# Twelve more contexts' keys and values computed inside level 0's self attention, early contexts spread over the batch, and level 3's steps reordered

## The chip, the core and the metric

The kernel runs on one core of one Trainium2 chip. The metric is device time in microseconds (us) for one execution of the whole program. The core has five engines, each with its own instruction sequence: TensorE (PE in the profile, with its weight loads as PEld), VectorE (DVE), ScalarE (ACT), GpSimd (POOL) and SyncE (SP, which here issues DMA transfers). They wait for one another by semaphores. Everything is computed in single precision, but for a few small whole-number tables.

## The reference

The program is a stack of four levels over 2048 rows of x (64 batch elements, called contexts below after the 64 context sequences they attend to, with 32 rows each) and a context of 257 rows per batch element, all 256 wide. Each level attends to the context (xattn), then to itself (attn), then has a feed-forward part (ffn):

```
B, T, S, D = 64, 32, 257, 256
x    [64, 32, 256]     ctx  [64, 257, 256]
x = l0_xattn(x, ctx); x = l0_attn(x); x = l0_ffn(x)
x = l1_xattn(x, ctx); x = l1_attn(x); x = l1_ffn(x)
x = l2_xattn(x, ctx); x = l2_attn(x); x = l2_ffn(x)
x = l3_xattn(x, ctx); x = l3_attn(x); x = l3_ffn(x)
```

Three parts matter here.

- Level 3's cross attention: for each batch element, k = ctx Wk + bk and v = ctx Wv + bv; queries from a layer norm of x; per head (16 heads of width 16) softmax(q k / 4) v, a projection, and a residual sum. The keys and values depend on the context and on weights alone, not on x, so they can be computed at any earlier time.
- Level 0's self attention: 16 heads of width 16 over the 32 rows of a batch element, with queries and keys of unit length, softmax, output projection, residual sum.
- Level 0's feed-forward: a mixture of eight experts in which each expert takes the 256 rows with the highest router probability.

## The kernel before

x stays in SBUF as 16 tiles of 128 rows (NT = 16), each holding four batch elements (NB = 4). The parts run one after the other; a scheduler orders instructions by their dependences and by memory, except within `as_written(...)`, where the named engines keep the order in which the code issues them.

**Early and late contexts.** Level 3's keys and values take four pieces of matmul work per context: two for keys (each 128x257 out), two for values (each 128x256 out). `l3_keys_values(one, ps, n)` (L1027) sets up a generator that does this for the next n contexts: it loads the weights `kv_w` (two DMAs on SP, L1033), loads each context's transpose (SP, L1042), and yields after every piece. ACT moves the pieces from PSUM to SBUF (L1056 and L1065) and issues the DMA that writes the finished keys and values to DRAM (`self.kv[b]`, 513 KB, L1066). `filled(n)` (L1071) runs the next n pieces, so that they stand in the gaps of whatever calls it. The generator is set up twice, for 16 contexts each: in level 0's feed-forward (L1169) and in level 1's feed-forward (L1655). Contexts 0 to 31 are therefore "early"; level 3 reads their keys and values back from DRAM. Contexts 32 to 63 are "late": level 3 loads the context and does the four pieces itself.

**Level 0's self attention** (`l0_attn`, L795) is a software pipeline over the 16 tiles, in which one iteration runs steps of several tiles: norm and query/key/value projection of tile i or i+1, unit length and `heads_first` of tile i-1 (four transposes into PSUM `m`; ACT copies them to `qT` and `kb`), `scores` and softmax of tile i-2 (PSUM `s`, four banks; DVE reads them twice, for the row maxima `hs_m` and for the difference `hs_e`), and `weighted` and `output` of tile i-3 (PSUM `o`). Its PSUM pool has one buffer of `m`, two of `qk`, one of `s` (four banks) and one of `o`, eight banks in all. The steps of all four compute engines are kept as written.

**Level 0's feed-forward** (`l0_ffn`, L1152) begins with eight DMAs of 1 MB on SP for the experts' weights (`w_all`, L1162) and with `probabilities` (L998): for each of 16 tiles a layer norm to `rt_n` (four buffers), a DMA of it to DRAM (`nd`), two transposes, a small matmul with the router's weights, and one `filled()`. Then `places` (L1108) finds each expert's 256th highest probability bit by bit, in 30 steps of compare, count on PE (`pl_m`), and a few small DVE operations, with one `filled()` a step and six behind. Only DVE keeps its written order in this whole part, and PE, DVE and ACT keep it within the 30 steps.

**Level 3's cross attention** (`l3_xattn`, L2641) is again a software pipeline, one context per iteration n, with PE, DVE and ACT kept as written. `loaded` brings keys and values or the context; `norm`, `turned` and `projected` make the queries for four contexts at a time; `scores` (PSUM `s`) is followed by the negative row maxima `nm` (DVE, L2788) and the exponentials `e` with their sums `ss` (ACT, L2789); `divided` takes `rs` = 1/`ss` (DVE, L2797) and multiplies (POOL, L2798); `keys_first` transposes e, evacuated as `eT` half by DVE and half by ACT; `weighted` multiplies with the values, and DVE picks and sums the own heads' part (`t`, `oT`, L2825 and L2831); `last_rows` and `output` finish a tile. `keys_values` does the four pieces of a late context.

Of the kernel before, what the change touches and what calls it, by code (L numbers as in the profile page):

```python
# [26 lines left out]
B, T, S, D = 64, 32, 257, 256  # L27
NT = B * T // 128
NB = 4
KP, KC = 96, 3  # L30
KL = S - 2 * KP
SP = KP * KC
# [291 lines left out]
class Perceiver:  # L324
    def __init__(self, ctx, tc, a):
        self.tc, self.nc, self.a = tc, tc.nc, a
        nc = self.nc
        self.n_tiles = 0
        self.const = ctx.enter_context(tc.tile_pool(name="const", bufs=1))
        self.wpool = ctx.enter_context(tc.tile_pool(name="weights", bufs=N_SLOTS))  # L330
        self.x = self.sb(self.const, [128, NT, D], "x")
        self.cols = self.sb(self.const, [128, N_COL], "cols")
        self.con = self.sb(self.const, [128, N_CON], "con")
        nc.sync.dma_start(self.cols, a["cols"])
        self.ident = self.sb(self.const, [128, 128], "ident")
        make_identity(nc, self.ident)
        self.neg_half = self.sb(self.const, [128, 1], "neg_half")
        nc.gpsimd.memset(self.neg_half, -0.5)
        self.seed = self.sb(self.const, [128, 1], "seed", I32)
        nc.gpsimd.memset(self.seed, RSQRT_SEED + 1)  # L340

        self.ctx_st = self.sb(self.const, [128, 2 * B, 6], "ctx_st")
        self.ctx_st_x = self.sb(self.const, [B, 1, 6], "ctx_st_x")


        self.k_wT = self.sb(self.const, [128, 6, D], "k_wT")
        self.c_mean = self.sb(self.const, [128, B, 2], "c_mean")
        self.c_rc = self.sb(self.const, [128, B, 2], "c_rc")
        self.nxT = self.sb(self.const, [128, 2, B], "nxT")
        dram = ctx.enter_context(tc.tile_pool(name="rows_d", bufs=1, space=bass.MemoryType.DRAM))  # L350
        self.abd = self.sb(dram, [B, 2, S], "abd")

        self.kv = self.sb(dram, [B, 128, 2 * S + 2 * D], "kv")
        self.n_kv = 0

    def forms(self, pool):
# [438 lines left out]
    def l0_attn(self):  # L795
        nc, tc, a = self.nc, self.tc, self.a
        wqkv = self.weight(a["l0a_wqkv"], 2)
        wo = self.weight(a["l0a_wo"], 4)
        with ExitStack() as st:
# [12 lines left out]
            def norm_1(i):  # L812
                st = self.sb(pool, [128, 6], "ln_st")
                nc.vector.bn_stats(st, self.x[:, i, :])
                mv = self.sb(pool, [128, 2], "ln_mv")
                nc.vector.bn_aggr(mv, st)
                t_n[i] = mv, self.rsqrt(pool, mv[:, 1:2], LN_EPS, "ln_r")
# [104 lines left out]
            def output(i):  # L922
                py = self.sb(ps, [128, D], "o")
                self.mm(py, [(t_o[i][:, k, :], wo[:, k, :]) for k in range(4)])
                nc.vector.tensor_tensor(self.x[:, i, :], self.x[:, i, :], py, ALU.add)

            norm_1(0), norm_2(0), turned(0)
            st.enter_context(self.as_written(nc.tensor, nc.vector, nc.scalar, nc.gpsimd))
            for i in range(NT + 3):
                steps = [  # L930
                    (i + 1, norm_1),
                    (i - 1, unit),
                    (i, projected),
                    (i, lambda t: lengths(t, 0)),
                    (i - 2, scores),
                    (i + 1, norm_2),
                    (i - 3, weighted),
                    (i - 1, heads_first),
                    (i - 2, divided),
                    (i, lambda t: lengths(t, 1)),  # L940
                    (i - 3, output),
                    (i + 1, turned),
                    (i - 2, diagonal),
                ]
                for t, step in steps:
                    if 0 <= t < NT and not (t == 0 and step in (norm_1, norm_2, turned)):
                        step(t)

    def heads_softmax(self, pool, src, bd, scale, plus=0.0):

# [73 lines left out]
        nc.vector.tensor_tensor(p, lg, bcast(ss, 2, 8), ALU.mult)  # L1024
        return p

    def l3_keys_values(self, one, ps, n):  # L1027


        nc, a = self.nc, self.a  # L1030
        w = self.sb(one, [128, 2, 2, D], "kv_w")
        for j in range(2):
            nc.sync.dma_start(w[:, j], a["l3x_w"][1 + j].rearrange("p (k n) -> p k n", k=2))  # L1033
        wk, wv = w[:, 0], w[:, 1]
        todo = range(self.n_kv, self.n_kv + n)
        self.n_kv += n
        ts = {}

        def loaded(b):
            if b in todo:  # L1040
                t = self.sb(self.wpool, [128, 2048], "w")
                nc.sync.dma_start(t[:, 0 : 2 * S], a["ctxT"][b])  # L1042
                ts[b] = t

        def steps():
            for b in todo[:2]:
                loaded(b)
            for b in todo:
                loaded(b + 2)
                t = ts.pop(b)  # L1050
                cT = t[:, 0 : 2 * S].rearrange("p (k s) -> p k s", k=2)
                kv = t[:, 2 * S : 4 * S + 2 * D]
                for o in range(2):
                    pk = self.sb(ps, [128, S], "h")
                    self.mm(pk, [(wk[:, k, o * 128 : (o + 1) * 128], cT[:, k, :]) for k in range(2)])
                    nc.scalar.activation(  # L1056
                        kv[:, o * S : (o + 1) * S], pk, AF.Identity, bias=self.col("L3_xattn_bk", o)
                    )
                    yield
                pv = self.sb(ps, [128, 2, D], "y")  # L1060
                for c in range(2):
                    self.mm(pv[:, c, :], [(cT[:, k, c * 128 : (c + 1) * 128], wv[:, k, :]) for k in range(2)])
                    if c == 0:
                        yield
                nc.scalar.copy(kv[:, 2 * S :], pv.rearrange("p c f -> p (c f)"))  # L1065
                nc.scalar.dma_start(self.kv[b], kv)  # L1066
                yield

        self.between = steps()
# [82 lines left out]
    def l0_ffn(self):  # L1152
        nc, tc, a = self.nc, self.tc, self.a
        wg = self.weight(a["l0f_wg"], 2)
        with ExitStack() as st:
# [10 lines left out]
            rows = st.enter_context(tc.tile_pool(name="l2r", bufs=1))  # L1166
            one1 = st.enter_context(tc.tile_pool(name="l0s", bufs=1))
            pool = st.enter_context(tc.tile_pool(name="l0f", bufs=3))
            self.l3_keys_values(one1, ps, 16)  # L1169
            p = self.probabilities(one, pool, ps, wg, None, nd)  # L1170
            st.enter_context(self.as_written(nc.vector))
            place = self.places(one, pool, ps, tab, p)
# [462 lines left out]
    def l1_ffn(self, ahead, last):  # L1635
# [4 lines left out]
        with ExitStack() as st:  # L1640
# [11 lines left out]
            sums = self.sb(dram, [NT * 128, D], "sums")  # L1652
            nc.scalar.dma_start(sums.rearrange("(i p) f -> p i f", p=128), self.x)
            xn = self.sb(dram, [NT * 128, R], "xn")
            self.l3_keys_values(one, ps, 16)  # L1655
            p = self.probabilities(one, pool, ps, wr, br, xn)
            nc.scalar.dma_start(xn.rearrange("(i p) f -> p i f", p=128)[:, :, D:R], p)
            place = self.places(one, pool, ps, tab, p)
# [982 lines left out]
    def l3_xattn(self):  # L2641
# [3 lines left out]
        with ExitStack() as st:  # L2645
# [100 lines left out]
                    )  # L2746

            def loaded(b):
                kv = self.sb(pool, [128, 2 * S + 2 * D], "kv", bufs=7)
                t_kv[b] = [kv[:, 0 : 2 * S].rearrange("p (k s) -> p k s", k=2), kv[:, 2 * S :].rearrange("p (c f) -> p c f", c=2)]  # L2750
                if b < self.n_kv:
                    nc.sync.dma_start(kv, self.kv[b])
                    return
                cT = self.sb(pool, [128, 2, S], "cT", bufs=4)
                nc.sync.dma_start(cT, a["ctxT"][b].rearrange("p (k s) -> p k s", k=2))
                t_c[b] = cT

            def keys_values(b):
                if b < self.n_kv:
                    return  # L2760
                cT = t_c[b]
                kT, v = t_kv[b]
                for o in range(2):
                    pk = self.sb(ps, [128, S], "m")
                    self.mm(pk, [(wk[:, k, o * 128 : (o + 1) * 128], cT[:, k, :]) for k in range(2)])
                    nc.scalar.activation(kT[:, o, :], pk, AF.Identity, bias=self.col("L3_xattn_bk", o))
                pv = self.sb(ps, [128, 2, D], "m")
                for c in range(2):
                    self.mm(pv[:, c, :], [(cT[:, k, c * 128 : (c + 1) * 128], wv[:, k, :]) for k in range(2)])
                nc.vector.tensor_copy(v, pv)  # L2770

            def scores(b):
# [9 lines left out]
                            [(qb[f, c, bl].rearrange("p h t -> p (h t)"), kT[f, c, :])],  # L2782
                        )
                nm = self.sb(pool, [128, 4], "nm")
                e = self.sb(pool, [128, 4, S], "e")
                ss = self.sb(pool, [128, 4], "ss")
                for r in range(4):
                    nc.vector.tensor_reduce(nm[:, r : r + 1], pss[r], AX.X, ALU.max, negate=True)  # L2788
# [44 lines left out]
                )  # L2833

            st.enter_context(self.as_written(nc.tensor, nc.vector, nc.scalar))
            for n in range(-5, B + 6):

                steps = [(loaded, n + 3, 1), (norm, n + 4, NB), (scores, n, 1), (keys_values, n + 1, 1)]
                steps += [(divided, n, 1), (turned, n + 3, NB), (projected, n + 2, NB)]
                steps += [(weighted, n - 2, 1), (keys_first, n - 1, 1), (last_rows, n - 4, NB), (output, n - 8, NB)]  # L2840
                if n == -4:
                    row_values()
                for step, at, per in steps:
                    if at % per == 0 and 0 <= at < B:
                        step(at // per)
# [95 lines left out]
```

## Time and profile before

| | us |
|---|---|
| median of 3 runs | 3927.5 |
| lowest and highest of them | 3921.29, 3932.42 |
| the profiled execution | 3939.03 |
| its span in the profile | 3937.3 |

The mean granted TensorE clock of the profiled execution is 0.955 of full speed. Over the span the engines are busy as follows:

| engine | busy us | share |
|---|---|---|
| PE | 3546.4 | 90% |
| PEld | 2794.3 | 71% |
| DVE | 1963.4 | 50% |
| POOL | 1387.9 | 35% |
| ACT | 1293.2 | 33% |

The parts that the change touches stand in these stretches of the span: level 0's self attention from 388 to 588 us, level 0's feed-forward up to its expert slots from 588 to 694 us, and level 3's cross attention from about 3190 to 3595 us.

How to read it: a timeline line gives start and length in us, the engine, the line of the code, the operation, what it writes and reads by the program's names with its shape, and how many such instructions were joined (x4). A bracket at the end gives how long the engine had been idle before, and what released it. One matmul of single precision shows as two or more records. In a table of windows each engine's busy time is followed by its number of records, and PEclk is the clock granted to TensorE as a share of full speed. A busy share over the whole span averages stages with different limits, so each stage is looked at by itself.

### The profile page before, as it was taken

How to read it: one execution, taken by the hardware profiler on the slowest of the kernel's cores; microseconds unless marked ns; L12 is line 12 of the kernel's file. 1: busy time of each engine (PE TensorE's matmuls, PEld its weight loads, DVE VectorE, ACT ScalarE, POOL GpSimd, SP SyncE). 2: the span in 40 equal slices, each digit the busy share in tenths (PEclk: the TensorE clock that was granted, in tenths of full speed). 3: DMA queues.
4: the chain of work that ended last, by engine and by line, in shares of the span. 5: the costliest groups of instructions: out<-in, count | busy, mean ns of one | idle time of the engine just before them, and what ended most of it. 6: DMA issues, size and time to landing. Idle time of an engine off the chain costs nothing.

```text
span 3937.3 us, 74907 instructions
## 1 busy us (share of the span) xinstructions
PE 3546.4 (90%) x29677; PEld 2794.3 (71%) x29677; DVE 1963.4 (50%) x5180; ACT 1293.2 (33%) x3551; POOL 1387.9 (35%) x1752
## 2 busy tenths in 40 slices
PE   7999778879899789799999899979999987998998
PEld 5788446756577667577777566669999965776776
DVE  5555665234344441677766466632222246554454
ACT  2333223423233132333333243322222235543332
POOL 5433751133311113555655244451121135333121
PEclk9999889989999889899999899999999989999999
DMA  6342007256100265333333000010000133110000
GB/s 211 124 153 87 8 7 257 89 188 208 50 2 2 80 184 166 107 91 84 86 85 93 25 1 2 23 66 1 1 1 1 44 102 101 37 42 22 7 7 12
DMA packets 176413, 281.11 MB, mean 71 GB/s; under 512 B 33536, under 2 KB 109824, under 8 KB 171840
## 3 DMA queue, kind: packets, MB, share of 16 engines
q1 hardware_dynamic: 155472, 239.58, 19.7%
q10 hardware_dynamic: 14976, 25.01, 1.8%
q0 software_dynamic: 5616, 11.74, 1.3%
q8 instruction: 236, 3.87, 0.4%
q14 instruction: 113, 0.93, 0.1%
HBM read 243.46 MB, written 32.79 MB: 70 GB/s over the span
## 4 chain that ended last, share of the span: by engine, by line
PE 72%; DVE 11%; POOL 6%; ACT 5%; issue 3%; DMA 2%; ACTq 0%; SPq 0%; DVEq 0%; POOLq 0%
PE m L471 32%; PE p L471 10%; PE s L471 5%; PE y L471 3%; PE h L471 3%; PE b L471 3%; PE o L471 3%; PE ab L471 2%; ACT e L2789 2%; DVE bd L970 2%; PE y L476 2%; PE k L471 1%; PE c L471 1%; POOL e L2798 1%; PE m L465 1%
## 5 line engine op out<-in xcount | busy, mean ns | idle before, releaser
L471 PE MATMUL m<-w,oT 128*128 128x256 f32 x1152 | 272.8, 387 | 23.4 <-ACT eT L2809 15.2
L471 PEld LDWEIGHTS m<-w,oT 128*128 128x128 f32 x1152 | 219.9, 194 | 63.1 <-ACT eT L2809 17.0
L471 PE MATMUL m<-nTg,w 128*128 128x256 f32 x1024 | 234.7, 387 | 4.3 <-ACT k L1520 2.9
L471 PEld LDWEIGHTS m<-nTg,w 128*128 128x128 f32 x1024 | 193.3, 192 | 35.6 <-ACT k L1520 4.9
L2798 POOL TENSOR_TENSOR e<-e,rs 128x1028 f32<-128x1028 f32 x64 | 121.7, 1902 | 200.2 <-DVE rs L2797 200.2
L471 PE MATMUL s<-cT,ut 128*128 128x257 f32 x768 | 181.1, 386 | 0.0
L471 PE MATMUL m<-pT,cn 128*128 128x384 f32 x512 | 176.2, 487 | 2.5 <-DVE pT L2174 2.5
L2151 ACT ACTIVATE p<-s,bi 128x257 f32<-128x257 f32 x192 | 88.9, 472 | 247.0 <-DVE bi L2147 226.7
L423 POOL TENSOR_SCALAR ln_r_v<-ln_mv 128x1 f32<-128x1 f32 x176 | 38.7, 223 | 348.1 <-DVE ln_mv L454 266.3
L471 PEld LDWEIGHTS s<-cT,ut 128*128 128x128 f32 x768 | 143.5, 193 | 19.4 <-ACT p L2151 0.2
L2789 ACT ACTIVATE e<-s,nm 128x257 f32<-128x257 f32 x256 | 118.1, 474 | 113.4 <-DVE nm L2788 93.1
L970 DVE STREAM_TRANSPOSE bd<-hs_p 32x512 f32<-32x512 f32 x192 | 134.8, 702 | 40.2 <-POOL hs_p L964 37.0
L2120 POOL TENSOR_TENSOR cT<-cT,ab 128x514 f32<-128x514 f32 x64 | 82.4, 1288 | 205.4 <-PE m L471 85.8
L471 PEld LDWEIGHTS m<-pT,cn 128*128 128x128 f32 x512 | 96.5, 189 | 58.7 <-DVE pT L2174 2.9
L2255 POOL TENSOR_TENSOR sr<-ss,neg_half 128x16 f32<-128x16 f32 (+1 forms) x33 | 95.0, 2879 | 113.1 <-DVE ss L2253 113.1
L471 PE MATMUL m<-w,nT 128*128 128x512 f32 (+2 forms) x320 | 126.2, 536 | 8.8 <-ACT nT L829 8.2
L2545 POOL TENSOR_TENSOR tB<-hB 128x512 f32<-128x512 f32 x8 | 10.2, 1271 | 326.2 <-ACT hB L2583 326.2
L471 PE MATMUL ab<-nTg,w 128*128 128x256 f32 x512 | 117.1, 388 | 6.5 <-DVE hA L2561 5.5
L471 PE MATMUL m<-w,nTg 128*128 128x512 f32 x256 | 117.7, 604 | 0.0
L471 PEld LDWEIGHTS ab<-nTg,w 128*128 128x128 f32 x512 | 98.2, 194 | 23.3 <-DVE hA L2561 9.2
L2160 POOL TENSOR_TENSOR p<-p,rs 128x771 f32<-128x771 f32 x64 | 95.2, 1488 | 46.7 <-DVE rs L2159 27.9
L471 PE MATMUL o<-bd,v 128*64 128x128 f32 (+1 forms) x1536 | 90.1, 287 | 21.4 <-DVE bd L970 21.4
(712 smaller groups left out, 8819.9 us busy)
## 6 DMA issues: line engine op xcount, KB each, us to landing
ct<-in_ctx SPq DMA_DIRECT2D x192, 256.0 KB
cT<-in_ctxT SPq DMA_DIRECT2D x32, 1028.0 KB
cT<-in_ctxT SPq DMA_DIRECT2D x96, 257.0 KB
ab<-abd SPq DMA_DIRECT2D x64, 257.0 KB
kv<-w ACTq DMA_DIRECT2D x32, 513.0 KB
kv<-kv SPq DMA_DIRECT2D x32, 513.0 KB
rb<-rd SPq DMA_DIRECT2D x16, 514.0 KB
w<-in_ctxT SPq DMA_DIRECT2D x32, 257.0 KB
```

The lines of the kernel that those rows point to most:

```text
L423: nc.gpsimd.tensor_scalar(t, src, eps, None, ALU.add)
L465: self.nc.tensor.transpose(out[:, c, :], src[:, c * 128 : (c + 1) * 128], self.ident)
L471: self.nc.tensor.matmul(out, lhsT=l, rhs=r, start=j == 0, stop=j == last)
L476: self.nc.tensor.matmul(out[:, 0:n], lhsT=cT[0], rhs=self.k_qm[:, 0, 0:n], start=True, stop=False)
L970: self.nc.vector.transpose(bd[q, :, b, :], p[q])
L2120: nc.gpsimd.tensor_tensor(cT, cT, bcast(ab[:, 0, :], 1, 2), ALU.mult)
L2151: nc.scalar.activation(p[:, g, :], pss[g], AF.Exp, bias=bi[:, g : g + 1], accum_out=ss[:, g : g + 1])
L2160: nc.gpsimd.tensor_tensor(p, p, bcast(rs, 2, S), ALU.mult)
L2255: nc.gpsimd.tensor_tensor(r, ss, self.neg_half[:p].to_broadcast([p, nh]), ALU.pow)
L2545: nc.gpsimd.tensor_tensor(t1, b12, b11, ALU.subtract)
L2789: nc.scalar.activation(e[:, r, :], pss[r], AF.Exp, bias=nm[:, r : r + 1], accum_out=ss[:, r : r + 1])
L2798: nc.gpsimd.tensor_tensor(e, e, bcast(rs, 2, S), ALU.mult)
```

## The change

- Instead of the first 32, 44 contexts are early, and they are spread over the batch: of each 16, all but the numbers 0, 3, 6, 9 and 12. Twenty contexts stay late.
- The 12 additional ones are done within `l0_attn`. The pieces take the scores' PSUM banks `s` (one tile of four banks for a context: two for keys, one for both value pieces) and four SBUF buffers `kv_t` of that part. Each iteration runs two pieces after `heads_first`, one after `output` and one after `turned`, for i = 1 to 12.
- `l3_keys_values` gets its PSUM banks and its buffers from the caller. The two places that had it keep their own banks (`h`, `h`, `y`) and 16 contexts each.
- In `l3_xattn` the order of the steps changes: `weighted` and `keys_first` go ahead of `divided` and are done one iteration later, as are `last_rows` and `output`; the loop is two iterations longer. There are eight buffers of `kv` in place of seven and four of `e` in place of three.

The order of instructions that results also differs where no line of the diff stands: `l0_attn` takes more memory, and the start of `l0_ffn`, which had run within it (four `rt_n` and their writes to `nd`, and the DMAs of `kv_w`), comes after it; `kv_w` stands on SP behind the eight loads of `w_all`, and 16 of the pieces that stood one per tile in `probabilities` stand together between the first and the second step of `places`.

```diff
+EARLY = 44
+        self.early = [b for b in range(B) if (b + 1) * EARLY // B > b * EARLY // B]
...
+            banks = {}
+            def bank(j):
+                if j == 0:
+                    banks["s"] = self.sb(ps, [128, 4, 512], "s")
+                return banks["s"][:, j, :]
+            self.l3_keys_values(
+                one, 12, bank, lambda: self.sb(one, [128, 4 * S + 2 * D], "kv_t", bufs=4)
+            )
             norm_1(0), norm_2(0), turned(0)
...
                     (i - 1, heads_first),
+                    (i - 1, lambda t: self.filled(2)),
                     (i - 2, divided),
                     (i, lambda t: lengths(t, 1)),
                     (i - 3, output),
+                    (i - 1, lambda t: self.filled(1)),
                     (i + 1, turned),
+                    (i - 1, lambda t: self.filled(1)),
                     (i - 2, diagonal),
...
+            self.filled(4 * B)
...
-    def l3_keys_values(self, one, ps, n):
+    def l3_keys_values(self, one, n, bank, buf=None):
...
-        todo = range(self.n_kv, self.n_kv + n)
+        todo = self.early[self.n_kv : self.n_kv + n]
...
-                    pk = self.sb(ps, [128, S], "h")
+                    pk = bank(o)[:, 0:S]
...
-                pv = self.sb(ps, [128, 2, D], "y")
+                pv = bank(2)
...
-            self.l3_keys_values(one1, ps, 16)
+            self.l3_keys_values(one1, 16, lambda j: self.sb(ps, [128, 512], "hhy"[j]))
...
-                kv = self.sb(pool, [128, 2 * S + 2 * D], "kv", bufs=7)
+                kv = self.sb(pool, [128, 2 * S + 2 * D], "kv", bufs=8)
...
-                if b < self.n_kv:
+                if b in self.early:
...
-                e = self.sb(pool, [128, 4, S], "e")
+                e = self.sb(pool, [128, 4, S], "e", bufs=4)
...
-            for n in range(-5, B + 6):
+            for n in range(-5, B + 8):
                 steps = [(loaded, n + 3, 1), (norm, n + 4, NB), (scores, n, 1), (keys_values, n + 1, 1)]
-                steps += [(divided, n, 1), (turned, n + 3, NB), (projected, n + 2, NB)]
-                steps += [(weighted, n - 2, 1), (keys_first, n - 1, 1), (last_rows, n - 4, NB), (output, n - 8, NB)]
+                steps += [(turned, n + 3, NB), (projected, n + 2, NB), (weighted, n - 3, 1)]
+                steps += [(keys_first, n - 2, 1), (divided, n, 1), (last_rows, n - 5, NB), (output, n - 9, NB)]
```

More of the change, by code (lines that the diff above doesn't have):

```diff
@@ L1039, in loaded @@
         def loaded(b):
[L1040 to L1043, printed above, removed]
+            t = buf() if buf else self.sb(self.wpool, [128, 2048], "w")
+            nc.sync.dma_start(t[:, 0 : 2 * S], a["ctxT"][b])
+            ts[b] = t
         def steps():
@@ L1047, in steps @@
                 loaded(b)
-            for b in todo:
-                loaded(b + 2)
+            for at, b in enumerate(todo):
+                for c in todo[at + 2 : at + 3]:
+                    loaded(c)
                 t = ts.pop(b)
@@ L1059, in steps @@
                     yield
-                pv = self.sb(ps, [128, 2, D], "y")
+                pv = bank(2)
                 for c in range(2):
-                    self.mm(pv[:, c, :], [(cT[:, k, c * 128 : (c + 1) * 128], wv[:, k, :]) for k in range(2)])
+                    self.mm(
+                        pv[:, c * D : (c + 1) * D],
+                        [(cT[:, k, c * 128 : (c + 1) * 128], wv[:, k, :]) for k in range(2)],
+                    )
                     if c == 0:
                         yield
-                nc.scalar.copy(kv[:, 2 * S :], pv.rearrange("p c f -> p (c f)"))
+                nc.scalar.copy(kv[:, 2 * S :], pv)
                 nc.scalar.dma_start(self.kv[b], kv)
@@ L1654, in l1_ffn @@
             xn = self.sb(dram, [NT * 128, R], "xn")
-            self.l3_keys_values(one, ps, 16)
+            self.l3_keys_values(one, 16, lambda j: self.sb(ps, [128, 512], "hhy"[j]))
             p = self.probabilities(one, pool, ps, wr, br, xn)
@@ L2758, in keys_values @@
             def keys_values(b):
-                if b < self.n_kv:
+                if b in self.early:
                     return
```

## The prediction, made before the changed kernel had run

> **What bounds the kernel now.** I began with the chain of waits over the whole span, to see which engine sets the end, and then cut the span into the stages that the change touches.
>
> ```profile
> PE 72%; DVE 11%; POOL 6%; ACT 5%; issue 3%; DMA 2%; ACTq 0%; SPq 0%; DVEq 0%; POOLq 0%
> ```
>
> TensorE carries 72% of the chain, so matmuls taken out of one stage and put into another pay only where the first stage is bound by TensorE and the second is not. The table of windows says which is which; its columns are length, busy PE, weight load, DVE, ACT and POOL, granted clock, DMA share, GB/s.
>
> ```profile
> 388.00:588.00 200.00, 144.47 (x1896) 94.41 (x1896) 127.99 (x264) 57.04 (x129) 132.46 (x100) 0.87 0.03 10
> 588.00:694.00 106.00, 82.42 (x413) 63.10 (x412) 56.62 (x241) 32.43 (x68) 11.89 (x23) 0.89 0.75 257
> 3200.00:3360.00 160.00, 126.46 (x1359) 89.20 (x1356) 102.70 (x275) 85.14 (x320) 84.10 (x100) 0.92 0.32 98
> 3360.00:3583.00 223.00, 221.72 (x1926) 175.04 (x1922) 132.32 (x317) 111.69 (x379) 85.09 (x99) 1.00 0.15 42
> 450.00:470.00 20.00, 16.58 (x133) 10.51 (x132) 12.87 (x27) 4.61 (x11) 12.79 (x11) 0.68 0.03 9
> 480.00:540.00 60.00, 44.44 (x709) 30.11 (x708) 47.14 (x99) 21.24 (x48) 47.60 (x37) 1.00 0.01 2
> ```
>
> Row 1 is level 0's self attention: PE is busy 72%. Row 2 is level 0's feed-forward up to its expert slots. Rows 3 and 4 are level 3's cross attention with its 32 early and its 32 late contexts: 5.0 us a context with gaps, then 6.97 us with none (221.72 of 223). Rows 5 and 6 show one and the same loop of self attention at two clocks.
>
> **Keys and values inside self attention.** A context is four pieces; dense at full clock one takes 0.87 us (eight records in 1.74 us, 667.61 to 669.35 below). Twelve iterations, i = 1 to 12, take one context each. In rows of the timeline, an iteration at full clock:
>
> ```profile
> 534.30 0.69 DVE L893 TENSOR_TENSOR hs_e<-s,hs_m 128x512 f32<-128x512 f32 x1
> ...
> 536.24 1.99 PE L471 MATMUL o<-w,oT 128*128 128x256 f32 x8 [2.08 <-ACT oT L919]
> ...
> 538.27 0.42 DVE L925 TENSOR_TENSOR x<-x,o 128x256 f32<-128x256 f32 x1 [1.55 <-PE o L471]
> ```
>
> PE is done with the heads-first transposes at 534.17, then waits 2.08 us for the output's oT. That gap looks free, but the pieces write the scores' banks, and DVE reads these until 534.99 (534.30 + 0.69). So PE is held 0.8 us first. Walked from 534.99: two k pieces to +1.8, output to +3.85 (before +3.25: 0.6 late), a v piece to +4.7, the turn, a v piece to +6.0, projection to +8.85 (before +6.95). The squares, ms and the next scores follow 1.9 late, and the next hs_e ends at +11.75, against a loop of 10.03 us now. Behind the waiting piece on PE stand output, turn and projection; x (DVE), and behind it the four bd transposes, wait for output.
>
> Twelve iterations take 130.7 us now (kb from 405.8 to 536.5), since several ran at the clock of row 5. After: about 10 + 11 + 10 x 11.75 = 138.5 at full clock, **+8**. Packed PE would be the floor: 44.44 us in six iterations is 7.41, plus 3.48, is 10.89 each, 130.7 for twelve, **0**. Slow stretches kept as they are (130.7 / 120.4 for twelve at 10.03), 138.5 becomes 150, **+20**. Here I weigh the Trainium skill, "TensorE: Matmul & The Clock Gate", "What's actually happening": TensorE runs at half clock until a busy stretch of some microseconds frees it, and idle ones throttle it again. By the rule a filled loop never cools, and +8 holds. By the rows it is not that plain: row 5 is busier (16.58 of 20) than row 6 (44.44 of 60) because its matmuls are slow. Nearer the rule, as fill removes idle time: **+11**.
>
> A rule against the change: "Perfetto Trace Analysis", "Optimizing Tensor Performance", says that independent matmul groups should rotate through different PSUM banks so that one's evacuation overlaps the next. The row above is its price: pieces in other banks would start at 534.17, the loop would be about 10.9, twelve iterations some 10 us shorter and the term about 0. The pool (m 1, qk 2, s 4, o 1) leaves no bank, so I keep the row's sum.
>
> ACT's two Identity evacuations and a copy (about 0.5 us each) fit in its 64% idle; 12 writes of 0.5 MB stand against 2 GB/s.
>
> **What moves in level 0's feed-forward.** Self attention now takes more memory, and the order of instructions shows that nothing of the feed-forward overlaps it any more. The weights kv_w of its own keys and values are now issued on SP behind eight 1 MB loads:
>
> ```profile
> 387.56 0.81 SPq L1033 DMA_DIRECT2D kv_w<-in_l3x_w  x2
> ...
> 588.90 29.33 SPq L1162 DMA_DIRECT2D w_all<-in_l0f_w  x8
> ```
>
> so they come near 620, when the 16 tiles of the router's normalization (588.9 to 622.4) are nearly done. That stretch is bound by DMA (DVE's rt_n waits 11.3 us in three waits for the write of nd, beside 257 GB/s), so its 16 pieces were free there. After, 16 of them stand together between the first two steps of the search for places, ahead of every later step on PE.
>
> ```profile
> 625.16 2.03 PE L471 MATMUL h<-w,kv_w 128*128 128x257 f32 x4
> ...
> 667.61 1.90 PE L471 MATMUL h<-w,kv_w 128*128 128x257 f32 x8
> ```
>
> Each later step of 1.35 us hides one piece already, and 667.6 to 682.5 is dense with fill, so there is no slack left to catch up in. Sixteen pieces: 16 x 0.87 = 13.9, plus 1.7 for a half-clock start (625.16: four records take 2.03, not 0.87). Four contexts' writes (2.1 MB, 7 us at 300 GB/s) leave the router's stretch, while the four normalizations that ran inside self attention join it: a gain of up to 7 or a loss of 3. The feed-forward: **+15**, ends +5 and +19.
>
> **Level 3.** The intervals between reciprocals rs are the clock of a context. Early group of four now: 6.8, 4.15, 4.2, 6.1 (20.5 on average); late group 28.2; first to last rs 379.5 us (3203.9 to 3583.4).
>
> ```profile
> 3269.42 0.18 DVE L2797 RECIPROCAL rs<-ss 128x4 f32<-128x4 f32 x1 [1.09 <-ACT e L2789]
> ...
> 3271.06 1.41 DVE L2788 TENSOR_REDUCE nm<-s 128x1 f32<-128x257 f32 x4
> 3273.56 0.18 DVE L2797 RECIPROCAL rs<-ss 128x4 f32<-128x4 f32 x1 [1.09 <-ACT e L2789]
> ...
> 3281.06 0.41 DVE L458 TENSOR_SCALAR n<-x,ln_mv,ln_r 128x256 f32<-128x256 f32 x1 [1.01 <-POOL ln_r L425]
> ```
>
> This is DVE's loop: rs, then t, oT and eT (1.64 us), nm, and 2.5 us from nm's start to the next rs through ACT's exponentials. The new order puts t, oT and eT between nm and rs, beside the exponentials: 3.15 instead of 4.15. Two intervals of four do not follow: the one with turned, projected and output is bound by PE (5.9), and the one with the norm still goes rs, statistics, POOL (behind its 1.9 us product), n, nm: 6.7. An early group is then 3.15 + 5.9 + 3.15 + 6.7 = 18.9, little below 19.7, its value now at full clock.
>
> A late context adds 3.67 us on PE where PE binds, 3.25 on a 3.15 interval, only 0.55 on the norm's. Spread, the five late ones of 16 contexts fall on all positions (b = 0, 3, 6, 9, 12, computed an iteration ahead): about 14. So 16 contexts take 4 x 18.9 + 14 = 89.7; four times that, less the last norm, is about 357 against 379.5. The early half's clock is 0.92 now; if such gaps spread over all 64, add 6 to 10: 357 to 367, a gain of 12 to 22. Context 0 is now late and its keys go ahead of the first scores: +3 to 4. The loop's two more iterations issue nothing on their own, and an eighth kv and a fourth e buffer only ease waits. Twelve more reads of kv (0.5 MB) on SP replace smaller ones of ctxT against 42 to 98 GB/s. Taken: **-13**; ends -18 and -4.
>
> **The sum**: 11 + 15 - 13 = **+13** on the execution profiled, 3939.03 us (span 3937.3, 1.7 around it), so 3952. The median of the runs, 3927.5, lies 0.29% lower: **3940**.
>
> **Rivals.** About 0.3% (12 us) is what a measurement of this kernel tells from no change.
> - *Forecast*, 3940, own range 3927 to 3955. For it: row 4 has no slack, yet the early half, with the same PE work less 3.67 us, already ran at 5 us, not 3.3. Chance **0.52**.
> - *Level 3 packs*: the spread contexts fill the norm's and the DVE loop's stalls, so PE binds all along. Its work, 126.46 + 221.72 less 12 x 3.67, is some 304 us; with a few stalls 325, a gain of 55, net -29: 3898. It decides from where the norm's interval falls from 6.7 to about 4.5. For: half clock inflated 126.46. Against: the rs-to-nm chain is untouched. Chance **0.13**.
> - *Every term at its floor*: self attention +0 (PE packed), feed-forward +5, level 3 -18: -13, 3914. Chance **0.17**.
> - *The stalls stay cold*: self attention +20, feed-forward +17, level 3 -6: +31, 3958. For: clocks of 0.68 and 0.92 in stages full of gaps. Chance **0.18**.
> - That the change doesn't compute 12 contexts ahead is excluded by the order of instructions.
>
> The forecast's cases split about 0.24 within 0.3% and 0.28 above, the floor's 0.12 below and 0.05 within. Faster 0.25, same 0.29, slower 0.46. The range 3906 to 3962 leaves out the packed case and thin edges.
>
> **What would show it.** The loop of self attention between kb's: 11.7 us, with a piece waiting for hs_e. Sixteen pieces in a lump after 625 and the expert slots some 15 us later from the stage's start. Intervals of rs in level 3 near 3.2, 5.9, 3.2, 6.7, and first to last rs near 360. It is wrong if that last figure is under 340 or over 372, or if self attention's loop stays at 10.

## The result, and the profile after

The changed kernel takes 3971.43 us (median of 4 runs, 3968.64 to 3979.5) against 3927.91 us of before (4 runs, 3921.29 to 3932.42): a ratio of 1.0116, 95% interval 1.0094 to 1.0137. It is slower, by 43.5 us. The execution profiled has a span of 3977.5 us, 40.2 more than the span before. Both profiled executions lie above the median of their runs, by 8.1 and by 11.1 us.

Where these 40 us come from is read by marks: the same instruction is looked up in both traces, and the distance between its two start times is the offset so far. Each mark is an instruction of DVE or ACT that both kernels have.

| mark | before | after | offset | this stage |
|---|---|---|---|---|
| self attention, kb of tile 0 | 405.8 | 403.0 | -2.8 | |
| self attention, kb of tile 12 | 536.5 | 566.1 | +29.6 | |
| self attention, kb of tile 15 | 566.1 | 596.7 | +30.6 | **+33.4** |
| feed-forward, end of the router (rt_l) | 622.4 | 647.5 | +25.2 | -5.4 |
| feed-forward, a count after the lump (pl_cnt) | 627.3 | 674.4 | +47.1 | +21.9 |
| feed-forward, first expert's y | 703.4 | 754.2 | +50.9 | +3.8, together **+20.3** |
| level 2's self attention (ss) | 2546.3 | 2601.2 | +54.9 | +4.0 |
| level 3, first rs | 3203.9 | 3263.1 | +59.2 | +4.3 |
| level 3, last rs | 3583.4 | 3619.7 | +36.3 | -22.9 |
| last row of level 3's self attention | 3917.0 | 3957.4 | +40.4 | +4.1, level 3 together **-14.5** |

So the moved work gives back 14.5 us where it was taken out, and costs 53.7 where it was put in. The table of windows of the changed kernel, with the columns as before (length; busy PE, weight load, DVE, ACT, POOL, each with its records; granted clock; DMA share; GB/s):

```profile
388.00:588.00 200.00, 163.89 (x1824) 115.62 (x1825) 108.83 (x211) 70.18 (x156) 119.68 (x79) 0.92 0.16 54
588.00:694.00 106.00, 76.89 (x497) 59.27 (x495) 46.19 (x163) 21.84 (x48) 17.80 (x37) 0.68 0.47 164
...
3263.00:3619.00 356.00, 325.64 (x3029) 239.47 (x3027) 221.13 (x573) 183.71 (x663) 168.51 (x198) 0.91 0.26 76
```

The first two windows are the stretches shown of before. In the first, PE is now busy 82% of the time instead of 72, and yet DVE has less done (211 instructions, 264 before): the tiles advance more slowly. In the second the stage now begins 31 us later, and the clock is 0.68 where it was 0.89.

**Self attention.** The timeline of one iteration of the changed kernel, at full clock:

```profile
523.24 0.69 DVE L896 TENSOR_TENSOR hs_e<-s,hs_m 128x512 f32<-128x512 f32 x1
...
524.03 1.11 PE L474 MATMUL s<-kv_t,kv_w 128*128 128x257 f32 x4 [0.61 <-PE m L2502]
...
525.40 0.84 ACT L869 ACTIVATE kb<-m,kw 128x256 f32<-128x256 f32 x2
...
526.11 0.49 ACT L1075 ACTIVATE kv_t<-s,cols 128x257 f32<-128x257 f32 x1
...
526.65 1.14 PE L474 MATMUL s<-kv_t,kv_w 128*128 128x257 f32 x4 [1.51 <-ACT kv_t L1075]
...
527.63 1.89 PE L474 MATMUL o<-w,oT 128*128 128x256 f32 x8
...
529.55 0.42 DVE L928 TENSOR_TENSOR x<-x,o 128x256 f32<-128x256 f32 x1 [3.89 <-PE o L474]
```

The first key piece starts as soon as hs_e has read the scores' banks, as foreseen. The second does not follow it: PE sits idle for 1.51 us until ACT has copied the first piece (kv_t), and ACT does so only after hs_e's exponential, oT, qT and kb. Two key pieces that go to two banks of one PSUM tile have become a round trip over ACT. The pieces also share an SBUF tile with the copies (kv_t, from which they read the context and into which ACT writes), but that is not what holds them: in the feed-forward, shown below, two key pieces share the tile w in the same way, have a PSUM tile h each, and follow one another without a wait. The output's matmuls, ready since oT, are queued on PE behind the second piece. These are PE's waits from kb of tile 0 to kb of tile 12, with total, number of times and longest:

```profile
PE s L474 <- ACT kv_t L1075: 17.9, 14, 1.5
PE s L474 <- PE m L2502: 6.1, 10, 0.6
```

The intervals between kb are now 13.0 us, and each second or third is 14.6 or 14.7: there the piece behind the wait runs at half clock (2.08 us for four records at 512.08, 1.14 here).

**The feed-forward.** kv_w's two transfers are issued on SP after w_all, land later than expected, and PE waits for them. First the rows of SP, then those of PE with one of ACT:

```profile
620.25 23.96 SPq L1184 DMA_DIRECT2D w_all<-in_l0f_w  x8
644.26 6.30 SPq L1052 DMA_DIRECT2D kv_w<-in_l3x_w  x2
```

```profile
650.21 0.27 PE L474 MATMUL m<-pl_m,rt_ones 128*128 128x128 bf16 x1 [2.72 <-DVE pl_next L1146]
656.67 3.80 PE L474 MATMUL h<-w,kv_w 128*128 128x257 f32 x8 [6.20 <-DMA kv_w<-in_l3x_w]
...
658.80 0.47 ACT L1075 ACTIVATE w<-h,cols 128x257 f32<-128x257 f32 x1 [9.99 <-PE h L474]
...
673.29 1.03 PE L474 MATMUL h<-w,kv_w 128*128 128x257 f32 x4
674.16 0.22 PE L474 MATMUL m<-pl_m,rt_ones 128*128 128x128 bf16 x1
```

The eight records at 656.67 are two key pieces back to back, while ACT copies the first of them at 658.80. From the first to the second step of places (the two rows with pl_m) it takes 23.95 us: a wait of 6.2 and 17 pieces. Before, it was 1.88 us, with one piece between:

```profile
625.11 0.26 PE L471 MATMUL m<-pl_m,rt_ones 128*128 128x128 bf16 x1 [2.78 <-DVE pl_next L1124]
625.16 2.03 PE L471 MATMUL h<-w,kv_w 128*128 128x257 f32 x4
626.99 0.31 PE L471 MATMUL m<-pl_m,rt_ones 128*128 128x128 bf16 x1
```

The router itself ends 5.4 us sooner against the stage's start, without fill beside it.

**Level 3.** A late context in the new order, from the timeline: the PE rows are its keys, its values, the queries, and then weighted.

```profile
3360.37 2.00 PE L474 MATMUL m<-cT,w 128*128 128x257 f32 x8
...
3362.21 1.89 PE L474 MATMUL m<-w,cT 128*128 128x256 f32 x8
...
3362.76 0.21 ACT L2811 ACTIVATION_READ_ACCUMULATOR e<-s,nm 128x1 f32 x1
...
3363.94 1.05 PE L474 MATMUL m<-nT,w 128*128 128x128 f32 x8
...
3364.92 1.15 PE L474 MATMUL m<-eT,kv 128*64 128x128 f32 x16
...
3366.11 0.42 DVE L2847 TENSOR_TENSOR t<-m,own 128x256 f32<-128x256 f32 x1 [1.27 <-PE m L474]
...
3367.68 0.17 DVE L2819 RECIPROCAL rs<-ss 128x4 f32<-128x4 f32 x1
```

The sums that rs needs are there at 3362.97, when ACT has read its last accumulator; rs runs at 3367.68. It stands on DVE behind t, oT and eT, these wait for weighted, and weighted stands on PE behind the late context's four pieces. The next nm stands behind rs. So a step that was to take work off DVE's loop ties the loop to PE wherever a context is late.

### The profile page after: what moved, and what is told of

Same layout as the page of the kernel before. It is cut to its first block, busy times and chain, and to the rows that moved or that the text cites. A ratio compares the mean times of both kernels' runs of the same rounds, so it can differ in the third digit from the quotient of the medians.

```text
span 3977.5 us, 74948 instructions
## 1 busy us (share of the span) xinstructions
PE 3580.8 (90%) x29677; PEld 2818.8 (71%) x29677; DVE 1961.0 (49%) x5168; ACT 1300.5 (33%) x3563; POOL 1384.3 (35%) x1752
## 4 chain that ended last, share of the span: by engine, by line
PE 73%; DVE 11%; POOL 5%; ACT 5%; issue 3%; DMA 3%; SPq 0%; ACTq 0%; DVEq 0%; POOLq 0%
PE m L474 31%; PE p L474 10%; PE s L474 7%; PE y L474 3%; PE h L474 3%; PE b L474 3%; PE o L474 3%; PE ab L474 2%; PE y L479 1%; PE k L474 1%; PE c L474 1%; DVE bd L988 1%; PE m L468 1%; PE y L480 1%; PE m L1479 1%
```

## Experiments

Each run is compared with the kernel before in the same series of runs; the span and the marks are those of its profiled execution. The change itself has the ratio 1.0116.

**1. Both key pieces ahead of their copies.**

```diff
-                for o in range(2):
-                    pk = bank(o)[:, 0:S]
-                    self.mm(pk, [(wk[:, k, o * 128 : (o + 1) * 128], cT[:, k, :]) for k in range(2)])
+                pks = {}
+                for o in range(2):
+                    for j in range(2) if buf else [o]:
+                        if j not in pks:
+                            pks[j] = bank(j)[:, 0:S]
+                            self.mm(pks[j], [(wk[:, k, j * 128 : (j + 1) * 128], cT[:, k, :]) for k in range(2)])
+                    pk = pks[o]
                     nc.scalar.activation(
```

> Only the twelve contexts in self attention are touched: both key matmul pieces are issued before the two copies that evacuate them, so the second piece no longer waits for ACT's copy of the first. Theory (that wait, not the matmuls, makes the loop 13.0 us and more, and its idle PE lets the clock fall): the loop goes to about 11.7 us, kb of tile 0 to kb of tile 12 from 163 to about 141 us, the kernel to about 3950. Rival (the hold of the scores' banks until hs_e, plus PE's own work, sets the loop): it stays at 13 or more, the kernel at 3968 to 3974.

Measured: 3943.67 us, ratio 1.0048 (1.0031 to 1.0064). The loop is 11.22 us in every iteration from tile 2 on, and kb of tile 0 to tile 12 takes 135.9 us instead of 163.1. Below, first PE's rows, then its waits from kb of tile 0 to tile 12:

```profile
514.26 0.66 PE L2506 MATMUL m<-ident,qk 128*128 128x128 f32 x4
515.53 1.98 PE L474 MATMUL s<-kv_t,kv_w 128*128 128x257 f32 x8 [0.61 <-PE m L2506]
517.34 1.89 PE L474 MATMUL o<-w,oT 128*128 128x256 f32 x8
```

```profile
PE s L474 <- PE m L2506: 6.1, 10, 0.6
PE s L474 <- ACT kv_t L1079: 1.9, 2, 0.9
```

The wait for ACT is gone but for 1.9 us, the hold until hs_e (0.6 a time) is as it was, banks and work are unchanged. The rival falls: neither the hold nor PE's work made the loop 13.0 us long. Of the 27 us, an estimated 12 x (13.0 - 11.22) = 21 are the round trip, and the rest is the half clock, which went with it. The table of windows has the granted clock from 430 to 560 us, first in the change, then in this run:

```profile
430.00:560.00 130.00, 110.09 (x1233) 81.33 (x1234) 72.39 (x140) 47.03 (x105) 72.17 (x47) 0.95 0.15 50
...
430.00:560.00 130.00, 118.34 (x1558) 87.72 (x1556) 91.07 (x175) 54.02 (x122) 87.40 (x57) 0.99 0.16 56
```

**2. Nothing in self attention, 32 contexts early.** The call of `l3_keys_values` and every `filled` go from `l0_attn`:

```diff
-EARLY = 44
+EARLY = 32
...
-            self.l3_keys_values(
-                one, 12, bank, lambda: self.sb(one, [128, 4 * S + 2 * D], "kv_t", bufs=4)
-            )
...
-                    (i - 1, lambda t: self.filled(2)),
...
-                    (i - 1, lambda t: self.filled(1)),
...
-            self.filled(4 * B)
```

> Nothing is computed ahead inside self attention: 32 contexts are early (spread, every second one), the level 3 order and buffers stay those of the change. Theory: self attention and the feed-forward behind it return to the times of before (50 us less), level 3 has twelve more late contexts at 2.5 to 3.3 us each: first to last rs about 390 us, the kernel about 3950. Rival (spread late contexts fill level 3's stalls): first to last rs 350 to 365, the kernel 3905 to 3920.

Measured: 3967.75 us, ratio 1.0105 (1.0088 to 1.0122). The first levels return to the times of before (offset -2.6 at the first expert's y, where the change has +50.9), so all that was lost there belongs to the moved pieces and the memory that they take. But first to last rs takes 412.1 us, more than either theory allowed, at a clock of 0.89: a late context costs far more in the new order than I had thought. That pointed to the order, which the next runs take up.

**3. The weights ahead of the 1 MB loads.** In `l0_ffn`, only the place of one call:

```diff
+            self.l3_keys_values(one, 16, lambda j: self.sb(ps, [128, 512], "hhy"[j]))
             w = self.sb(one, [128, 8, 2048], "w_all")
...
-            self.l3_keys_values(one1, 16, lambda j: self.sb(ps, [128, 512], "hhy"[j]))
```

> Only the place of one load is changed: the feed-forward's kv_w goes ahead of the eight 1 MB loads on SP. Theory (late weights make the lump): the pieces go back among the router's tiles, PE's wait of 6.2 us for kv_w and about 15 pieces (14 us) between the first two steps of places are gone, the writes of kv cost the router's stretch 5 us back: 13 to 18 us less, the kernel 3954 to 3958. Rival (the lump only takes the place of a wait for the expert weights or the gathers): the expert slots start no earlier, the kernel 3969 to 3973.

Measured: 3959.64 us, ratio 1.0080 (1.0061 to 1.0099), 12 us less than the change, just short of the theory's 13 to 18. The lump is gone: from the first to the second step of places it takes 1.87 us (661.10 to 662.97 in its timeline). The router's stretch takes part of it back, with fill and writes beside it again: its end stands at +36.0, the first expert's y at +42.5 (the change: +25.2 and +50.9).

**4. Level 3's old order**, with 44 contexts spread and the change's buffers.

```diff
-            for n in range(-5, B + 8):
+            for n in range(-5, B + 6):
...
-                steps += [(turned, n + 3, NB), (projected, n + 2, NB), (weighted, n - 3, 1)]
-                steps += [(keys_first, n - 2, 1), (divided, n, 1), (last_rows, n - 5, NB), (output, n - 9, NB)]
+                steps += [(divided, n, 1), (turned, n + 3, NB), (projected, n + 2, NB)]
+                steps += [(weighted, n - 2, 1), (keys_first, n - 1, 1), (last_rows, n - 4, NB), (output, n - 8, NB)]
```

> The change with level 3's steps in the old order (44 contexts early and spread, buffers as in the change). Theory (the new order takes a microsecond off the intervals that DVE bounds): first to last rs 365 to 375 us instead of 356.6, the kernel 3980 to 3990. Rival (fewer and spread late contexts made all of the gain): rs within 3 us of 356.6 and the kernel at 3971.

Measured: 3954.09 us, ratio 1.0071 (1.0055 to 1.0088): *faster* than the change by 17 us, against both theories. First to last rs takes 346.4 us instead of 356.6. In the profiled execution another 11.8 us of the lead stand already before the first rs, where both kernels have the same code: 4.9 us before self attention (kb of tile 0 at 398.1, in the change at 403.0; from there to tile 12 both take 163.1), the rest by the first expert's y and the first rs. So single executions of one code differ by that much here, and what the order is worth is read from level 3 alone. The same place as above, in the old order:

```profile
3346.79 0.21 ACT L2811 ACTIVATION_READ_ACCUMULATOR e<-s,nm 128x1 f32 x1
...
3347.89 0.17 DVE L2819 RECIPROCAL rs<-ss 128x4 f32<-128x4 f32 x1
...
3349.24 0.42 DVE L2847 TENSOR_TENSOR t<-m,own 128x256 f32<-128x256 f32 x1 [1.19 <-PE m L474]
```

rs follows its sums after 0.9 us, not 4.7, and t waits behind it.

**5. What of the new order costs it.** The change with one step put back:

```diff
-                steps += [(turned, n + 3, NB), (projected, n + 2, NB), (weighted, n - 3, 1)]
-                steps += [(keys_first, n - 2, 1), (divided, n, 1), (last_rows, n - 5, NB), (output, n - 9, NB)]
+                steps += [(divided, n, 1), (turned, n + 3, NB), (projected, n + 2, NB)]
+                steps += [(weighted, n - 3, 1), (keys_first, n - 2, 1), (last_rows, n - 5, NB), (output, n - 9, NB)]
```

> The change with one step of level 3 put back: divided (and with it rs on DVE) stands again ahead of weighted and keys_first, which stay one iteration later. Theory (in the new order rs waits on DVE behind t, oT and eT, and these behind a late context's matmuls on PE): first to last rs 342 to 350 us instead of 356.6, the kernel 3952 to 3962. Rival (the later iteration of weighted and keys_first is what costs): rs stays at 354 to 358, the kernel at 3968 to 3973.

Measured: 3958.51 us, ratio 1.0076 (1.0064 to 1.0089), and rs in 343.2 us. The place of divided is the whole cost of the new order, 13 us in this kernel (from the mark in level 2 to the end of level 3 the offset changes by -27.5 us here and by -14.5 in the change); doing weighted and keys_first one iteration later costs nothing between the rs (343.2 against 346.4 in the old order).

**6. The spread alone**: the diffs of runs 2 and 4 together.

> Nothing inside self attention, 32 early contexts, the old order of level 3, but early contexts spread (every second one) and the change's buffers: the spread alone. Theory (spread late contexts fill level 3's stalls): first to last rs 355 to 370 us against 379.5, the kernel 3910 to 3920. Rival (a late context costs its full 3 us wherever it stands): 376 to 382 us, the kernel 3923 to 3931.

Measured: 3927.84 us, ratio 0.9992 (0.9983 to 1.0002). Rs takes 369.8 us, so the spread fills some stalls, as the theory has it; but the whole kernel can't be told from before, as the rival has it. The rs leave out level 3's two ends. From the mark in level 2 to the last row of level 3's self attention the gain is 0.8 us: of the 9.7 between the rs, 4.7 are lost before the first rs (context 0 is now late, for which the prediction had 3 to 4) and 4.2 after the last. Against run 2, where only the order differs, the loop of rs is 42 us shorter at a clock of 0.99 instead of 0.89: the more contexts are late, the more the new order costs.

**7. The three edits together**: the diffs of runs 1, 3 and 4.

> The three edits tried one at a time are put together: both key pieces ahead of their copies, the feed-forward's kv_w ahead of the 1 MB loads, and level 3's old order, with 44 contexts early and spread. Theory (three separate costs in three stages): the single effects, 28, 12 and 17 us, add up to 57, so 3912 to 3918, faster than before. Rival (they draw on the same slack, or the old order's gain was mostly scatter of self attention's clock): 3924 to 3932, no faster than before.

Measured: 3919.95 us, ratio 0.9978 (0.9971 to 0.9985), between the two expectations. The three ratios by themselves are 0.68, 0.36 and 0.45 points below the change's, 1.49 together; measured are 1.38. They add up nearly, so they are three separate costs, and without them the change is faster than before by 0.2%.

**8. The first 44 contexts early**, otherwise as run 7.

```diff
-        self.early = [b for b in range(B) if (b + 1) * EARLY // B > b * EARLY // B]
+        self.early = list(range(EARLY))
```

> As the three parts together, but the first 44 contexts are early instead of spread ones. Theory (the spread makes part of the gain): eleven early groups of 20.5 us and five late of 28.2 us, first to last rs about 366 us against 346 spread, the kernel about 20 us slower than the three parts together. Rival (only the number of late contexts counts): within 4 us of it.

Measured: 3924.7 us, ratio 0.9986 (0.9977 to 0.9994); rs in 353.1 us. The spread is worth 6.6 us of rs, not 20, and 3.6 from the mark in level 2 to the end of level 3. The whole kernel has 4.8 us, with intervals that overlap: the theory's 20 falls, the rival's 4 is not excluded. My 366 was added up wrongly: it took the first and the last group at full length, while the same sum for before gives 390 where 379.5 were measured.

**9. divided ahead**: the diffs of runs 1, 3 and 5 together.

> Both key pieces ahead of their copies, kv_w ahead of the 1 MB loads, and of level 3's new order all but divided, which stands ahead of weighted. Theory (rs behind t, oT and eT was the whole cost of the new order): first to last rs 342 to 345 us against 346.5 with the old order, the kernel 3913 to 3919. Rival (the two added iterations at the end take the 3 us back): 3919 to 3923, no faster than with the old order.

Measured: 3921.57 us, ratio 0.9985 (0.9977 to 0.9993), rs in 343.5 us. Between the rs level 3 does what the theory said, but the kernel's time lies in the range of the rival. In the profile the 3 us are gone behind the last rs (that stretch is 3.7 us longer than before, 0.8 in run 7). The old order has 4.2 there in runs 4 and 6, so this is not shown to come from the two added iterations. Between runs 7 and 9 the whole kernel shows no difference.

**10. Sixteen contexts in self attention, 48 early**, otherwise as run 9.

```diff
-EARLY = 44
+EARLY = 48
...
-                one, 12, bank, lambda: self.sb(one, [128, 4 * S + 2 * D], "kv_t", bufs=4)
+                one, 16, bank, lambda: self.sb(one, [128, 4 * S + 2 * D], "kv_t", bufs=4)
```

> The run before with 16 contexts in self attention in place of 12, so that 48 are early and every fourth is late. Theory (a context costs self attention 1.2 us, as the loop of 11.22 against 10.03 shows, and a late one costs level 3 about 2.2 us): 4 more contexts give 4 us, first to last rs 330 to 336 us, the kernel 3909 to 3916. Rival (with every fourth late, all late ones fall on the same interval as the norm and cost nothing there): rs stays at 341 to 345, the kernel 3918 to 3924.

Measured: 3913.23 us, ratio 0.9957 (0.9944 to 0.9970), rs in 333.9 us. The loop of self attention stays at 11.22 us to the last tile. Late contexts are not free beside the norm; four fewer save 9.6 us of rs for some 6 in self attention (last kb at 571.9 against 565.4), of which 2.5 arise up to tile 12, where the code is the same. This is the fastest version run.

## Why the prediction was wrong

It gave 3940 us, 3906 to 3962; measured were 3971. By its steps:

- **Self attention, +11 predicted, +33 measured: the step that failed.** "Walked from 534.99: two k pieces to +1.8" put the two pieces back to back because their banks differ and PE was free, and ACT's copies were put at nothing because they "fit in its 64% idle". In the change the second piece waits for ACT's copy of the first, which stands behind hs_e, oT, qT and kb on ACT and ends at +2.7; the loop is 13.0 us, not 11.75. Run 1 takes that wait away, and nothing else: the loop is 11.22 us and the stage costs 5.0 us instead of 33.4, less than the +11 foreseen. The prediction had asked for each piece which bank it needs and when that is free, and not what else it waits for.
- **The clock.** The prediction leaned to +8 by the Trainium skill ("TensorE: Matmul & The Clock Gate", "What's actually happening"), which has idle stretches throttle TensorE again, and concluded that a filled loop stays warm. In the change it did not, with PE 82% busy; in run 1, without the hole of 1.51 us, it did. But the holes alone do not decide it. The change has holes of 1.51 and 0.61 us in 13.0 us and was granted 0.95; the loop of before has holes of 2.08 and 0.52 us in 10.03 us and was granted 1.00 from 480 to 540 us, and with holes of 2.4 and 0.5 us 0.68 from 450 to 470 us (the last two rows of windows in the prediction). What decides between the clocks is not shown by any run here.
- **The rule on banks** ("Perfetto Trace Analysis", "Optimizing Tensor Performance") was weighed against the wrong thing. The hold of the banks by hs_e came as priced (0.6 to 0.8 us an iteration), and run 1 pays it too. What cost was that evacuation and next group did not overlap *within* one tile, though in different banks.
- **The feed-forward, +15 predicted, +20.3 measured.** The mechanism was right. The mis-sized term is when kv_w lands: the wait of 6.2 us was not in the sum; "come near 620" becomes 651 with the stage's start 31 us later, and they were usable at 656.67, when the router was done and PE had nothing else. The lump's pieces came as counted (17 in 17.5 us), and the router gave 5 back, within the bounds. The 3.8 us after the lump are not explained; runs 4 and 5, with the same code there, do not have them (0.0 and -0.1), and their whole stage costs 16.8 and 17.6.
- **Level 3, -13 predicted, -14.5 measured**, and first to last rs 357 to 367 predicted, 356.6 measured. That the sum came out is in part luck. The walk had 89.7 us for each 16 contexts at full clock; at a clock of 0.91 the four stretches took 89.8, 95.6, 93.9 and, for the last 15 intervals, 77.4. Intervals of 3.0 to 3.6 did come, but in only 16 of 63. And the reason given was wrong: the new order was counted as a gain of one microsecond an interval, while with 44 spread contexts the old order takes 346.4 us and the new one 356.6. The walk had never been made for the old order, so it could not tell which half of the edit paid.
- Four us more appear between the feed-forward and level 2's mark, which the prediction did not have; in the other runs the same stretch has from -9.8 to +2.4, so they are taken for scatter. The 4 us at level 3's tail came in the old order as well (4.2 in runs 4 and 6, 0.8 and 0.2 in runs 7 and 8), so the order is not shown to be their cause; what is was not tried.

The rival "the stalls stay cold", 3958, had the right side and the right stage, but a different mechanism and 31 of the 43 us. The causes are settled for the wait in self attention (run 1), the lump in the feed-forward (run 3) and the order in level 3 (runs 4 and 5); what sets the clock stays open.

## What to carry to other kernels

Filling one engine's gaps with foreign work is paid by what that work waits for: list the waits of each filled piece, not only the engine's idle time, and issue all matmuls of a group ahead of the first copy that reads the tile they share. A step that a loop depends on (here the reciprocal that releases the next maxima) must not stand, on an engine whose instructions are kept as written, behind results of the engine that carries the extra work. And when an edit has two parts, walk each of them alone: a right sum can hide a part that loses.

## What was not expected of the hardware

- Two loops with holes at PE were treated differently by the clock: the one of before, 10.03 us with holes of 2.08 and 0.52, was granted 1.00 (480 to 540 us); that of the change, 13.0 us with holes of 1.51 and 0.61, though busier, 0.95 (430 to 560 us). Without the hole of 1.51 us it was 0.99 (run 1). In level 3 the new order was granted 0.91, the one with divided put back 0.96.
- Two transfers of 256 KB stood on SP behind 8 MB. From the start of the first's issue to the end of the second's it took 6.3 us (644.26 to 650.56), in which SP waited 5.5 us, and the data was usable at 656.67; in run 1 the same loads were usable 8.6 us after the start of their issue (617.81 to 626.39). Ahead of the 8 MB the two issues took 0.9 us (run 3).
